# Layer 2 of a four-layer network: norms with pixels on partitions, rounds in a pinned order, work handed to GpSimd and ScalarE; layer 0: other PSUM banks for its first units

## The chip, the core and the metric

The kernel runs on one core of a Trainium2 chip, in one launch. The metric is the device time of that launch in microseconds (us). Three runs of the kernel before gave 16575.54, 16579.15 and 16581.78 us; their median is 16579.15 us. The engines are named as in the profile: PE (TensorE; PEld is its weight load), DVE (VectorE), ACT (ScalarE), POOL (GpSimd) and SP (SyncE, which only issues transfers here).

## The reference, cut to what matters

The network has four layers on a tensor of 4 images, 96 channels and 56 x 56 = 3136 pixels, fp32 throughout. Each layer is applied to a group norm of the tensor and added to it. The change touches layer 0 (full attention with 3 heads of 16 dimensions) and layer 2.

```python
# layer 0, per image and head
attn = jax.nn.softmax(jnp.einsum('bhnd,bhmd->bhnm', q, k) * scale, axis=-1)
out = jnp.einsum('bhnm,bhmd->bhnd', attn, v)

# layer 2 (input: the group norm of x), per pixel p and the 15 x 15 window around it
x_n = x_flat / jnp.maximum(jnp.linalg.norm(x_flat, axis=-1, keepdims=True), 1e-12)
sims = jnp.where(valid, einsum(x_n[p], x_n[window of p]), -1e9)
top_sim, top_idx = jax.lax.top_k(sims, 8)
wts = jax.nn.softmax(top_sim, axis=-1)
agg = sum over k of wts[k] * x_flat[top_idx[k]]
x_ln = (x_flat - mean) / jnp.sqrt(var + 1e-05) * ln_w + ln_b     # over the 96 channels
enhanced = agg + x_ln
h = jax.nn.relu(enhanced @ w1.T + b1)
out = enhanced + h @ w2.T + b2
```

## The kernel before

The layers run one after another; each opens its own pools of tiles and closes them at its end, so that the next layer starts when the last one is done. Layers 1 and 3 are untouched by the change and take most of the time.

**Layer 2** works image by image (`for b in range(B)`). An image lies in SBUF as 96 partitions (channels) by 3136 pixels; `CH` is 448 pixels (7 chunks), `KT` is 112 pixels, two image rows (28 tiles). An image goes through four stages:

1. Group norm (`group_norm`, lines 88 to 110): seven statistics instructions, two tiny matmuls that average over groups of channels, a square root on ACT, and one scaling pass into `xf`.
2. Norms over the channels, which lie on partitions, chunk by chunk (lines 912 to 940). A square on ACT (L915, L932), a matmul with a 96 x 96 matrix of ones, which leaves the sum on every partition (L917, L926, L934), a square root on ACT (L919, L936), a reciprocal of the whole 96 x 448 chunk on DVE (L922, L938), and products on DVE. The results are `unit` (vectors of length 1) and `enh` (the layer norm, to which the attention is added). Then seven groups of four PE transposes make `ft`, the image with pixels on partitions (L947, L950).
3. Attention, 28 tiles of 112 queries (lines 953 to 1002). A tile needs the keys of its own and up to four tiles on both sides: `nt` is 9 in the middle and 5 to 8 near the image's top and bottom. PE makes the scores (L963); DVE adds the window mask and takes them out of PSUM (L967), finds the eight largest (L972), makes a copy in which these are replaced by a very small number (`left`, L974) and negates the maximum (L976); ACT takes three exponentials (L979 with the sum of the eight, L980 of all scores, L981 of `left`); DVE subtracts the last two (L983), so that only the eight weights are left, and makes a diagonal matrix of one over the sum (L985, L987); PE turns the weights, nine blocks of 112 x 112, with that diagonal as the other operand (L993), ACT copies them out of PSUM (L996), PE sums the nine products with `ft` (L999), and DVE adds the result to `enh` (L1002).
4. The two-layer perceptron, seven chunks (L1008, L1011, L1014, L1016, L1017), and a store issued by POOL (L1018).

The order on each engine is not written out in layer 2: the program order is the loop's, and the scheduler of the framework rearranges it, within what the tiles' numbers of buffers allow (two for most, one for `unit`). PSUM has eight banks: `psS` two tiles of two banks for scores, `psT` two of one bank for the turned weights, `psM` two of one bank for all else.

**Layer 0** is under `in_order(tc)`, which chains each instruction to the one before it on the same engine, so that the order of the program is the order of each engine. A unit is 128 queries by 448 keys of one head for all four images. Its scores are four matmuls with 32 rows each (`score`, L196), image `b` in row group `b`; DVE takes the maximum of each query (`largest`: L210 for a tile of two banks at once, L208 for one bank). The first `LEAD` = 160 units run ahead of everything else. Images 0 and 1 make one pair, 2 and 3 the other: of three pairs in turn, two get a `psE` tile of two banks, and the third gets two single banks of `psM`.

```python
if places % 3 < 2:
    p = psE.tile([128, 2, 512], F32, name="s")
    two = [p[:, 0], p[:, 1]]
    ps.append((bs[0], p))
else:
    two = [bank() for _ in bs]
    ps += zip(bs, two)
```

After a unit with n % 4 == 2, a block of other work is put in, 23 in all: 16 times `values` (L162) and 7 times `project` (L181), both of which use `psM` banks, as does `into_row` (L223) once in seven units. `psE` has two tiles (four banks), `psM` three banks, and `psA` one bank, for the accumulator that is used after the first 160 units.

## Time and profile before

| what | value |
|---|---|
| median of three runs | 16579.15 us |
| the profiled execution, its own time | 16544.92 us |
| its span | 16543.1 us |
| layer 2, from its first loads to its last store (9504 to 10604) | 1100 us |
| the first 160 units of layer 0 (64 to 486) | 422 us |
| busy in layer 2: DVE / PE / ACT / POOL | 843 / 856 / 541 / 15 us |
| table loads of ACT in layer 2 | 39 of 1283 ns |
| granted PE clock, whole span / layer 2 / the first 160 units | 0.91 / 0.86 / 0.56 |

The profiled execution is 34 us (0.2%) shorter than the median of the runs. Durations are taken from it, and sums are made against its own time. In the tables of groups, a row gives the line, engine and operation, the tiles written and read with their shapes, the number of instructions, the busy time with the mean of one in ns, and the engine's idle time just before them with what ended it. In the timeline a row gives the start, the duration, engine, line and operation; neighbouring instructions of one kind are merged. The stretches (windows) give the busy time of each engine in a stretch of the span, then the granted PE clock as a share of full speed.

### The profile page before, as it was taken

How to read it: one execution, taken by the hardware profiler on the slowest of the kernel's cores; microseconds unless marked ns; L12 is line 12 of the kernel's file. 1: busy time of each engine (PE TensorE's matmuls, PEld its weight loads, DVE VectorE, ACT ScalarE, POOL GpSimd, SP SyncE). 2: the span in 40 equal slices, each digit the busy share in tenths (PEclk: the TensorE clock that was granted, in tenths of full speed). 3: DMA queues.
4: the chain of work that ended last, by engine and by line, in shares of the span. 5: the costliest groups of instructions: out<-in, count | busy, mean ns of one | idle time of the engine just before them, and what ended most of it. 6: DMA issues, size and time to landing. Idle time of an engine off the chain costs nothing.

```text
span 16543.1 us, 501276 instructions
## 1 busy us (share of the span) xinstructions
PE 13366.7 (81%) x221976; PEld 8983.6 (54%) x221976; DVE 13918.8 (84%) x15345; ACT 12240.4 (74%) x15452; POOL 7665.0 (46%) x3968
## 2 busy tenths in 40 slices
PE   8999977777777777777776678778888888888866
PEld 4333325666666666666665445446666656666533
DVE  7666549999999999999998777768888888888866
ACT  0465449999999999999996244468888888888822
POOL 0000028888888888888885000023333333333300
PEclk6899889999999999999998588889999999999977
DMA  0000034334444434344445800122212222221122
GB/s 15 1 1 1 16 137 97 91 92 95 105 105 103 103 91 96 92 96 102 103 105 139 194 10 10 43 71 51 50 47 50 50 50 51 51 50 47 43 66 66
DMA packets 821402, 1152.50 MB, mean 70 GB/s; under 512 B 309360, under 2 KB 728720, under 8 KB 807456
## 3 DMA queue, kind: packets, MB, share of 16 engines
q1 hardware_dynamic: 759872, 1055.38, 26.3%
q10 hardware_dynamic: 53984, 45.77, 1.2%
q8 instruction: 1745, 28.59, 0.8%
q0 software_dynamic: 5376, 19.27, 0.4%
q14 instruction: 425, 3.48, 0.1%
HBM read 842.93 MB, written 277.18 MB: 68 GB/s over the span
## 4 chain that ended last, share of the span: by engine, by line
PE 32%; DVE 28%; ACT 19%; issue 15%; DMA 5%; SPq 1%; POOL 1%; DVEq 0%; ACTq 0%; POOLq 0%
DVE q L638 17%; PE q L1357 7%; ACT ht L663 5%; PE s L233 4%; ACT e L626 3%; PE d L417 3%; ACT phi L1305 3%; DVE w L1345 3%; PE z L1297 2%; PE acc L251 2%; PE m L196 2%; ACT w L1313 2%; PE t L561 2%; PE y L675 2%; DVE phi L1366 2%
## 5 line engine op out<-in xcount | busy, mean ns | idle before, releaser
L618 POOL TENSOR_TENSOR q<-du,bm 128x1792 f32<-128x1792 f32 x1344 | 5345.3, 4024 | 3.1 <-DMA bm<-bc 3.1
L638 DVE TENSOR_TENSOR_SCAN q<-e,state,q 128x448 f32<-128x448 f32 x4608 | 4874.1, 1122 | 142.7 <-ACT e L626 140.1
L626 ACT ACTIVATE e<-dl,na 128x448 f32<-128x448 f32 x5376 | 3355.4, 640 | 179.4 <-DVE q L638 123.7
L675 PE MATMUL y<-ht,cd 128*32 128x64 f32 x75264 | 1836.6, 225 | 1480.0 <-ACT ht L663 1479.5
L654 PE MATMUL t<-ident,q 128*128 128x128 f32 x18816 | 2611.9, 292 | 93.9 <-issue 77.8
L1357 PE MATMUL q<-w,m 32*32 32x192 f32 x52224 | 2573.2, 348 | 124.1 <-DVE phi L1366 71.2
L654 PEld LDWEIGHTS t<-ident,q 128*128 128x128 f32 x18816 | 2377.1, 203 | 324.4 <-issue 201.1
L663 ACT COPY ht<-t 128x896 f32<-128x896 f32 x2688 | 2428.3, 903 | 87.1 <-PE t L654 57.1
L675 PEld LDWEIGHTS y<-ht,cd 128*32 128x32 f32 x75264 | 1399.7, 110 | 1958.2 <-ACT ht L663 1942.9
L1357 PEld LDWEIGHTS q<-w,m 32*32 32x32 f32 x52224 | 1873.3, 113 | 737.7 <-issue 184.3
L1366 DVE TENSOR_TENSOR phi<-q,phi 128x768 f32<-128x768 f32 x1632 | 1512.4, 952 | 519.4 <-PE q L1357 491.7
L1378 POOL TENSOR_TENSOR t<-t 128x384 f32<-128x384 f32 x408 | 407.3, 998 | 2974.2 <-DVE t L1377 2974.2
L1297 PE MATMUL z<-ad,sm 32*32 32x256 f32 x39168 | 1277.4, 391 | 396.2 <-ACT phi L1305 382.0
L241 ACT ACTIVATE e<-s 128x896 f32<-128x896 f32 (+1 forms) x1050 | 921.7, 915 | 902.6 <-PE m L196 508.2
L1305 ACT COPY phi<-z 128x1536 f32<-128x1536 f32 x816 | 1164.5, 1427 | 526.5 <-PE z L1297 526.3
L208 DVE TENSOR_REDUCE pm<-m 128x1 f32<-128x448 f32 (+1 forms) x1672 | 982.9, 616 | 667.1 <-PE m L196 599.6
L1345 DVE TENSOR_TENSOR w<-w,misc 128x3072 f32<-128x3072 f32 x408 | 1364.8, 3345 | 82.7 <-PE misc L1329 47.0
L1313 ACT ACTIVATE w<-phi,lntiny,w_k_rmask 128x3072 f32<-128x3072 f32 x408 | 1203.1, 2949 | 2.6
L196 PE MATMUL m<-ka,qa 32*128 32x448 f32 (+1 forms) x3344 | 1169.3, 638 | 7.5 <-DVE pm L208 7.5
L1321 ACT ACTIVATE phi<-phi,w_k_nmask 128x3072 f32<-128x3072 f32 x408 | 1165.5, 2857 | 2.4
L1297 PEld LDWEIGHTS z<-ad,sm 32*32 32x32 f32 x39168 | 708.7, 104 | 659.6 <-ACT phi L1305 463.0
L292 POOL DMA_DIRECT2D x<-xc x28 | 14.5, 517 | 2178.4 <-DVE xc L291 2177.5
(255 smaller groups left out, 18928.9 us busy)
## 6 DMA issues: line engine op xcount, KB each, us to landing
bm<-bc SPq DMA_DIRECT2D x896, 448.0 KB
cm<-cd SPq DMA_DIRECT2D x544, 186.0 KB
l1y<-out SPq DMA_DIRECT2D x672, 96.0 KB
l1y<-out SPq DMA_DIRECT2D x672, 72.0 KB
y<-l1y ACTq DMA_DIRECT2D x224, 168.0 KB
l3y<-y SPq DMA_DIRECT2D x1616, 23.2 KB
w<-l3cr SPq DMA_DIRECT2D x408, 48.0 KB
l3cr<-phi SPq DMA_DIRECT2D x408, 48.0 KB
```

The lines of the kernel that those rows point to most:

```text
L618: nc.gpsimd.tensor_tensor(q, spread(s["du"][:, j, :], ng), s["bm"][g], ALU.mult)
L626: nc.scalar.activation(e[:, :CH], s["dl"][:, j, :], AF.Exp, scale=na[:, s["k"], j, n : n + 1])
L638: nc.vector.tensor_tensor_scan(a, e, a, first, ALU.mult, ALU.add)
L654: nc.tensor.transpose(flat(t)[:, 128 * c : 128 * c + 128], view(q, h * NC2 + c, [[NC, 128]]), self.ident,)
L663: nc.scalar.copy(t, flat(s["t", j, g, h])[:, : NC2 * 128])
L675: nc.tensor.matmul(s["y", j][r : r + 32, c // 4, 64 * half : 64 * half + 64], s["cd"][:, half, g, c, :], s["t", j, g, h][:, 128 * i + 64 * ...
L1297: nc.tensor.matmul(z[32 * b : 32 * b + 32, p, dh].rearrange("p n d -> p (n d)"), s["s"][ps_, dh, b, lo : lo + 32], st["ad"][ps_, dh, 8 * h ...
L1305: nc.scalar.copy(st["phi"][:, :, :, 8 * h : 8 * h + 8, :].rearrange("p a b n d -> p a b (n d)"), z.rearrange("p a b n d -> p a b (n d)"),)
L1313: nc.scalar.activation(w.rearrange("p a n d -> p (a n d)"), st["phi"].rearrange("p a b n d -> p (a b n d)"), AF.Sigmoid, bias=lntiny, scal ...
L1345: nc.vector.tensor_tensor(st["w"], st["w"], ut, ALU.mult)
L1357: nc.tensor.matmul(qp[bs, n, :DI], st["m"][bs, 4 * q + n, :], st["w"][bs, :, 4 * q + n, :], start=True, stop=True,)
L1366: nc.vector.tensor_tensor(ph, view(st[q], 0, [[256, 4], [32, 6], [1, 32]]), ph, ALU.mult)
```

## The change

In layer 2 the stages become functions, and the whole layer is put under `in_order`. The norms are made with pixels on partitions: the group norm is transposed first, mean and variance of each pixel come from the statistics instructions of DVE over the 96 channels, the factors for 112 x 28 pixels are worked out in a few small instructions, ACT scales by one over the length (`fu`), DVE subtracts the mean and scales (`fl`), and PE transposes both back to `unit` and `enh`. The matrix of ones, its matmuls and the reciprocals of whole chunks are gone.

The attention runs in rounds over four tiles at different stages: in round k the scores of tile k + 1, the selection for tile k, the exponentials of tile k - 1, and the turning and summing of tile k - 2. The subtraction of the two exponentials is issued to POOL, the diagonal to ACT. The group norm of the next image comes after an image's last round, the first half of its other norms between the chunks of the perceptron, and the second half after the last chunk. The perceptron takes its PSUM tiles from `psS` and `psT`.

In layer 0, the first 160 units take banks by turns: an even unit both `psE` tiles, an odd one the three `psM` banks and the one of `psA`. The four scores of a unit are issued together.

In the diff, the lines taken out of layer 2 are left out; they stand in the listing above.

```diff
@@ -299,20 +299,16 @@
                     project(0, c)
                 between = [lambda b=b, t0=t0: values(b, t0) for t0 in range(0, NT, 8) for b in range(B)]
                 between += [lambda c=c: project(1, c) for c in range(NCH)]
-                places = 0
                 for n, u in enumerate(units[:LEAD]):
-                    ps = []
-                    for bs in pairs:
-                        if places % 3 < 2:
-                            p = psE.tile([128, 2, 512], F32, name="s")
-                            two = [p[:, 0], p[:, 1]]
-                            ps.append((bs[0], p))
-                        else:
-                            two = [bank() for _ in bs]
-                            ps += zip(bs, two)
-                        places += 1
-                        for b, p in zip(bs, two):
-                            score(u, b, p)
+                    if n % 2 == 0:
+                        ps = [(bs[0], psE.tile([128, 2, 512], F32, name="s")) for bs in pairs]
+                        four = [p[:, i] for _, p in ps for i in range(2)]
+                    else:
+                        four = [bank() for _ in range(3)] + [psA.tile([128, 512], F32, name="acc")]
+                        ps = list(enumerate(four))
+                    for b, p in enumerate(four):
+                        score(u, b, p)
                     for b, p in ps:
                         largest(u, b, p)
                     if ended:
@@ -883,6 +879,8 @@
     def layer2(self, xin, xout):
         nc, tc = self.nc, self.tc
         with ExitStack() as cx:
             wp = cx.enter_context(tc.tile_pool(name="l2w", bufs=1))
@@ -896,50 +894,22 @@
                 self.load(wp, f"l2_{n}") for n in ("w1", "b1", "w2", "b2", "lnw", "lnb")
             )
             mask = self.load(wp, "k_window")
...
             def misc():
                 return psM.tile([128, 512], F32, name="misc")
...
+            def fetch(b):
                 x = sp.tile([C, L], F32, name="x")
                 nc.sync.dma_start(x, xin[b])
...
+                return dict(b=b, x=x)
+            def norms(s):
+                xf = s1.tile([C, L], F32, name="xf")
+                self.group_norm(s["x"], xf, ss, psM, "misc")
+                ft = s["ft"] = sp.tile([KT, NKT, C], F32, name="ft")
+                mv = sp.tile([KT, NKT, 2], F32, name="mv")
+                yield
                 for t0 in range(0, NKT, 4):
                     p = misc()
                     for i in range(4):
@@ -950,72 +920,172 @@
                     nc.scalar.copy(
                         ft[:, t0 : t0 + 4, :], p[:KT, : 4 * C].rearrange("p (t c) -> p t c", c=C)
                     )
...
+                    for t in range(t0, t0 + 4):
+                        st = ss.tile([KT, 6], F32, name="st", bufs=4)
+                        nc.vector.bn_stats(st, ft[:, t, :])
+                        nc.vector.bn_aggr(mv[:, t, :], st)
+                    yield
+                mu, var = mv[:, :, 0], mv[:, :, 1]
+                rn = sp.tile([KT, NKT], F32, name="rn")
+                rs = sp.tile([KT, NKT], F32, name="rs")
+                nc.vector.tensor_tensor(rn, mu, mu, ALU.mult)
+                nc.vector.tensor_tensor(rn, rn, var, ALU.add)
+                nc.scalar.activation(rn, rn, AF.Sqrt, scale=float(C))
+                nc.scalar.activation(rs, var, AF.Sqrt, bias=self.eps[:KT])
+                nc.vector.tensor_scalar(rn, rn, 1e-12, None, ALU.max)
+                nc.vector.reciprocal(rn, rn)
+                nc.vector.reciprocal(rs, rs)
+                unit = s["unit"] = s1.tile([C, L], F32, name="unit")
+                enh = s["enh"] = sp.tile([C, L], F32, name="enh")
+                for t0 in range(0, NKT, 4):
+                    fu = ss.tile([KT, 4, C], F32, name="fu")
+                    fl = ss.tile([KT, 4, C], F32, name="fl")
+                    for i in range(4):
+                        t = t0 + i
+                        nc.scalar.mul(fu[:, i, :], ft[:, t, :], rn[:, t : t + 1])
+                        nc.vector.tensor_scalar(
+                            fl[:, i, :], ft[:, t, :], mv[:, t, 0:1], rs[:, t : t + 1],
+                            ALU.subtract, ALU.mult,
+                        )
+                    cs = slice(t0 * KT, (t0 + 4) * KT)
+                    for f, o in ((fu, unit), (fl, enh)):
+                        p = misc()
+                        for i in range(4):
+                            nc.tensor.transpose(
+                                p[:C, i * KT : (i + 1) * KT], f[:, i, :], self.ident[:KT, :KT]
+                            )
+                        if o is unit:
+                            nc.vector.tensor_copy(o[:, cs], p[:C, :CH])
+                        else:
+                            nc.scalar.activation(o[:, cs], p[:C, :CH], AF.Identity, bias=lnb, scale=lnw)
+                    yield
+            def tile_of(s, i):
+                t0, t1 = max(0, i - 4), min(NKT - 1, i + 4)
+                return dict(
+                    s=s, t0=t0, nt=t1 - t0 + 1, m0=(t0 - i + 4) * KT, qs=slice(i * KT, (i + 1) * KT),
+                )
+            def scores(q):
+                hn = q["nt"] * KT // 2
+                unit = q["s"]["unit"]
+                p = q["p"] = psS.tile([KT, 2, 512], F32, name="s")
+                for a in range(2):
+                    k0 = q["t0"] * KT + a * hn
+                    nc.tensor.matmul(
+                        p[:, a, :hn], unit[:, q["qs"]], unit[:, k0 : k0 + hn], start=True, stop=True
                     )
...
+            def select(q):
+                n, m0 = q["nt"] * KT, q["m0"]
+                sm = q["sm"] = ss.tile([KT, 9 * KT], F32, name="sm", bufs=4)
+                nc.vector.tensor_tensor(
+                    sm[:, :n].rearrange("p (a k) -> p a k", a=2), q["p"][:, :, : n // 2],
+                    mask[:, m0 : m0 + n].rearrange("p (a k) -> p a k", a=2), ALU.add,
+                )
+                top = q["top"] = ss.tile([KT, 8], F32, name="top", bufs=3)
+                nc.vector.max(top, sm[:, :n])
+                nb = q["nb"] = ss.tile([KT, 1], F32, name="nb", bufs=3)
+                nc.vector.tensor_scalar(nb, top[:, 0:1], -1.0, None, ALU.mult)
+                left = q["left"] = ss.tile([KT, 9 * KT], F32, name="left", bufs=3)
+                nc.vector.match_replace(left[:, :n], top, sm[:, :n], -1.0e30)
+            def first_exps(q):
+                n, sm = q["nt"] * KT, q["sm"]
+                et = ss.tile([KT, 8], F32, name="et")
+                tot = q["tot"] = ss.tile([KT, 1], F32, name="tot", bufs=3)
+                nc.scalar.activation(et, q["top"], AF.Exp, bias=q["nb"], accum_out=tot)
+                nc.scalar.activation(sm[:, :n], sm[:, :n], AF.Exp, bias=q["nb"])
+            def second_exps(q):
+                n, sm, left = q["nt"] * KT, q["sm"], q["left"]
+                nc.scalar.activation(left[:, :n], left[:, :n], AF.Exp, bias=q["nb"])
+                nc.gpsimd.tensor_tensor(sm[:, :n], sm[:, :n], left[:, :n], ALU.subtract)
+            def scale(q):
+                rt = ss.tile([KT, 1], F32, name="rt")
+                nc.vector.reciprocal(rt, q["tot"])
+                dg = q["dg"] = ss.tile([KT, KT], F32, name="dg", bufs=3)
+                nc.scalar.mul(dg, self.ident[:KT, :KT], rt)
+            def turned(q, a0):
+                if a0 == 0:
+                    q["wt"] = ss.tile([KT, 9, KT], F32, name="wt")
+                m = min(4, q["nt"] - a0)
+                if m <= 0:
+                    return
+                p = psT.tile([KT, 4, KT], F32, name="pt", padded_shape=[KT, 4, 128])
+                for a in range(m):
+                    at = (a0 + a) * KT
+                    nc.tensor.matmul(p[:, a, :], q["sm"][:, at : at + KT], q["dg"], start=True, stop=True)
+                nc.scalar.copy(q["wt"][:, a0 : a0 + m, :], p[:, :m, :])
+            def sums(q):
+                s, nt = q["s"], q["nt"]
+                p = misc()
+                for a in range(nt):
+                    nc.tensor.matmul(
+                        p[:C, :KT], s["ft"][:, q["t0"] + a, :], q["wt"][:, a, :],
+                        start=a == 0, stop=a == nt - 1,
+                    )
+                enh = s["enh"][:, q["qs"]]
+                nc.vector.tensor_tensor(enh, enh, p[:C, :KT], ALU.add)
+            def mlp(s, c):
+                cs = slice(c * CH, (c + 1) * CH)
+                enh = s["enh"][:, cs]
+                hid = ss.tile([C, 2, CH], F32, name="hid")
+                p = psS.tile([KT, 2, 512], F32, name="s")
+                for a in range(2):
+                    nc.tensor.matmul(p[:C, a, :CH], w1[:, a * C : (a + 1) * C], enh, start=True, stop=True)
+                    nc.scalar.activation(hid[:, a, :], p[:C, a, :CH], AF.Relu, bias=b1[:, a : a + 1])
+                p = psT.tile([KT, 512], F32, name="po", tag="pt")
+                for a in range(2):
+                    nc.tensor.matmul(p[:C, :CH], w2[:, a, :], hid[:, a, :], start=a == 0, stop=a == 1)
+                o = ss.tile([C, CH], F32, name="o")
+                nc.vector.scalar_tensor_tensor(o, p[:C, :CH], b2, enh, ALU.add, ALU.add)
+                nc.vector.tensor_tensor(o, o, s["x"][:, cs], ALU.add)
+                nc.gpsimd.dma_start(xout[s["b"]][:, cs], o)
+            with in_order(tc):
+                s = fetch(0)
+                for _ in norms(s):
+                    pass
+                for b in range(B):
+                    following = fetch(b + 1) if b + 1 < B else None
+                    qs = [tile_of(s, i) for i in range(NKT)]
+                    scores(qs[0])
+                    for k in range(NKT + 2):
+                        new, now, mid, old = (
+                            qs[j] if 0 <= j < NKT else None for j in (k + 1, k, k - 1, k - 2)
+                        )
+                        if new is not None:
+                            scores(new)
+                        if old is not None:
+                            scale(old)
+                        if now is not None:
+                            select(now)
+                        if mid is not None:
+                            first_exps(mid)
+                        if old is not None:
+                            turned(old, 0)
+                        if mid is not None:
+                            second_exps(mid)
+                        if old is not None:
+                            turned(old, 4)
+                            turned(old, 8)
+                            sums(old)
+                    coming = norms(following) if following is not None else iter(())
+                    next(coming, None)
+                    for c in range(NCH):
+                        mlp(s, c)
+                        next(coming, None)
+                    for _ in coming:
+                        pass
+                    s = following
     def into_layer3(self, xin, dram):
```

## The prediction

> **What bounds the kernel now.** The page came first: its slices show DVE at nine tenths from slice 7 to 21. That is layer 1, which the change leaves alone. So I read the two stretches that it touches, by busy time in windows: all of layer 2, a steady piece of its attention, a piece of its norms, and the first units of layer 0.
>
> ```profile
> 9504.00:10604.00 1100.00, 855.53 (x4680) 552.39 (x4680) 843.45 (x1313) 541.19 (x1019) 14.89 (x30) 0.86 0.04 10
> 9649.40:9730.30 80.90, 74.05 (x522) 55.12 (x522) 68.83 (x117) 44.89 (x92) 0.00 (x0) 1.00 0.00 1
> 9520.00:9600.00 80.00, 47.60 (x90) 20.56 (x90) 67.63 (x84) 34.47 (x60) 0.00 (x0) 0.63 0.00 0
> 64.00:486.00 422.00, 414.42 (x1643) 200.47 (x1640) 337.61 (x470) 17.03 (x33) 0.00 (x0) 0.56 0.00 1
> ```
>
> Columns: stretch, length, busy PE, PEld, DVE, ACT, POOL, then the granted clock. DVE is busiest in the norms, DVE and PE are close in the attention, POOL does nothing. Then layer 2's groups on DVE, ACT and PE, and the steady attention's waits:
>
> ```profile
> L983 DVE TENSOR_TENSOR sm<-sm,left 112x1008 f32<-112x1008 f32 (+4 forms) x112 | 124.2, 1115 | 14.6 <-ACT left L981 14.6
> L938 DVE RECIPROCAL rn<-nr 96x448 f32<-96x448 f32 x28 | 82.5, 2947 | 35.8 <-ACT nr L936 35.8
> L922 DVE RECIPROCAL rn<-nr 96x448 f32<-96x448 f32 x28 | 82.4, 2942 | 0.1
> L987 DVE TENSOR_SCALAR dg<-ident,rt 112x112 f32<-112x112 f32 x112 | 31.0, 277 | 3.5
> L979 ACT ACTIVATE et<-top,nb 112x8 f32<-112x8 f32 x112 | 33.7, 301 | 29.1 <-DVE nb L976 28.6
> L999 PE MATMUL misc<-wt,ft 112*96 112x112 f32 x1856 | 219.4, 266 | 39.8 <-ACT wt L996 38.7 <-ACT ft L950 0.8
> ```
> ```profile
> PE misc L999 <- ACT wt L996: 6.8, 13, 0.5
> DVE rt L985 <- ACT et L979: 11.2, 13, 0.9
> ```
>
> Thirteen tiles take 80.9 us, 6.22 each. Neither engine is full: DVE waits 0.86 us a tile for ACT's exponential, PE 0.52 us for ACT's copy. It is a ring of queues, and the timeline of PE and ACT shows its parts:
>
> ```profile
> 9683.04 1.86 PE L963 MATMUL s<-unit 96*112 96x504 f32 x4
> 9684.81 2.13 PE L993 MATMUL pt<-dg,sm 112*112 112x112 f32 x18
> 9685.91 0.53 ACT L996 COPY wt<-pt 112x448 f32<-112x448 f32 x1 [2.77 <-PE pt L993]
> 9686.78 0.93 PE L999 MATMUL misc<-wt,ft 112*96 112x112 f32 x8
> 9688.22 1.15 ACT L981 ACTIVATE left<-left,nb 112x1008 f32<-112x1008 f32 x1
> 9688.24 1.20 PE L999 MATMUL misc<-wt,ft 112*96 112x112 f32 x10 [0.52 <-ACT wt L996]
> 9689.27 1.86 PE L963 MATMUL s<-unit 96*112 96x504 f32 x4
> ```
>
> From start to start: scores 1.77 us, turning 1.97, first sums 0.93, wait 0.53, last sums 1.03. PE alone would need 5.70 us.
>
> **Layer 2: the attention round.** DVE loses L983 (1.20 us at full width) and L987 (0.28); ACT gains the diagonal, POOL the subtraction. No row shows ACT's diagonal. Bounds: the copy of 112x112 by ACT takes 0.26 us; the line from L979 (8 elements, 0.30) to L981 (1008, 1.15) gives 0.39 at 112. I take 0.38. It costs nothing while PE makes scores (1.77 us); without that cover it would cost all 0.38.
>
> The order on each engine is now fixed, so a full round can be laid out from the row intervals above, t = 0 at PE's start of the scores:
> - DVE: add of the last tile at 0.25, reciprocal 0.42 to 0.59. ACT: diagonal 0.62 to 1.0, exponentials of eight and of all scores until 2.34.
> - PE: scores until 1.77, turning from 1.77. As at 9684.81 and 9685.91, the first copy follows 1.10 later, at 2.87.
> - ACT: that copy's slot 0.43, so `left` at 3.30, slot about 1.05; second copy at 4.35, done 4.88. In the order of before the second copy went ahead of `left`; now it is queued behind it.
> - PE: turning ends 3.74, first sums until 4.67, waits for the copy until 4.93, last sums until 5.96.
>
> The round is 5.96 us against 6.22. DVE's own queue (0.17 + 0.14 + 1.23 + 1.2 + 0.1 + 1.2 + 0.17) is 4.2 us and waits about 1.8 for the sums: the bound is now PE with ACT. POOL starts after `left`, at about 4.5.
>
> **POOL's price: row or rule.** The nearest row is POOL's product in layer 1:
>
> ```profile
> L618 POOL TENSOR_TENSOR q<-du,bm 128x1792 f32<-128x1792 f32 x1344 | 5345.3, 4024 | 3.1 <-DMA bm<-bc 3.1
> ```
>
> That is 2.25 ns an element; shorter ones (L1337, 496 elements, 1167 ns) give 2.35. For 1008 elements 2.35 us, and the ends are 2.1 (L1338's 2.05 ns) and 2.6 (L1378's). The turning that needs it starts at 5.96 + 1.77 = 7.73, and 4.5 + 2.35 = 6.85: hidden, with 0.9 us to spare. The Trainium skill speaks against it: its page "Perfetto Trace Analysis", section "Optimizing Scalar/DVE Operations", says that GpSimd and DVE share an SBUF read port, and that moving operations between those two might not help. Taken at its worst, all of DVE's 4.2 us and POOL's 2.35 exclude each other: 6.55 us a round, 0.59 x 112 tiles = 66 us more than my sum. But L618 keeps its 2.25 ns beside DVE's scans (L638 idles 142.7 / 4608 = 0.03 us before each), and of DVE's instructions in a round the add and the last add read one operand from PSUM. I take the row.
>
> **An image's attention.** Before the first turning the pipeline fills: scores of tile 0 and 1, two selections on DVE (2.5 and 2.9 us), about 7.4 us. Then rounds with narrow old tiles (5 to 8) of 4.9, 5.2, 5.5 and 5.8, twenty of 5.96, then 5.6, 5.2 and two without new scores, 4.4 and 3.4: 159 us. The last stage leaves PE's clock low. At 9605 to 9610 of the trace the clock is 0.50 although PE is busy, and 1.00 from 9610: some 4 us at half speed, 2 us lost. Sum 168 us.
>
> **Between two images.** Nothing of this now runs beside attention, as some of it did.
> - Group norm up to its second small matmul: 5.9 us with PE empty (the same chain at 10615.7 to 10621.1 takes 5.4). The rest lies beside the perceptron.
> - Seven chunks, perceptron and transposes in one queue: 3.15 us for the matmuls (8 of 0.37, and a wait for the first L1011; alone the chunk took 3.48 with its order) and 0.5 for four transposes (four take 0.85 at half clock, 0.4 at full): 25.6 us, and 1.5 for the cold start. DVE beside it: 1.3 for L1016 and L1017, and four times statistics and their aggregation. Those of 112x192 take 0.338 and 0.169; for 96 columns, on the slope to 96x448 (0.608), 0.24 + 0.17 with a short wait, 0.42: 1.7. Together 3.0 of 3.65, hidden.
> - The last statistics 2.4 us, then the small instructions for 3136 factors, about 1.1. ACT needs one square-root table here, loaded ahead, in place of the many switches.
> - Second half, seven chunks: on ACT four scalings of 112x96 (bounds 0.26 as above and 0.39, slot 0.28) 1.2 us; transposes at half clock and latency 0.45; DVE's copy is beside it; transposes of `fl` 0.65 more; ACT's scaling out of PSUM, 0.65. Near 2.95 a chunk, 20.6 us, with nothing beside it.
> Together 57 us.
>
> **Sum of layer 2.** Loads as before 12; image 0 alone: group norm 8.3, statistics 13.4 (7 x 1.7 and a start), 1.1, 20.6, that is 43; four attentions 672; three stages between, 171; the last perceptron 24 (it took 25.7). Sum 922 us against 1098 to the last store: 175 saved. DVE's bill agrees in kind. Per image it had 211 us of work; 98 go (reciprocals 41.2, L983 31.0, L987 7.8, the products and maxima of the norms 18), 24 come (28 statistics pairs, 28 scalings, 7 copies).
> The stores stay on POOL's queue; they are issued in the perceptron, when no subtraction is left, so the 0.51 us of each costs nothing. The load of the next image moves ahead of the attention on SP's queue, where nothing else stands.
>
> **Layer 0.** DVE's two kinds of maximum, and why it idles:
>
> ```profile
> L210 DVE TENSOR_REDUCE pm<-s 128x2 f32<-128x896 f32 x214 | 224.5, 1083 | 69.0 <-PE s L196 37.7 <-PE m L196 31.3
> L208 DVE TENSOR_REDUCE pm<-m 128x1 f32<-128x448 f32 x212 | 121.4, 613 | 26.8 <-PE s L196 26.2 <-PE m L196 0.6
> ```
>
> Its idle 96 us are the 23 blocks: one of `values` holds PE 3.6 us and DVE then stands 4.28. Of 320 pairs, 214 were wide; now it is 160 wide and 320 single: 160 x 1.049 + 320 x 0.573 = 351 us against 346, 5 more. With eight banks in place of seven, a block finds about 1 us more of maxima already scored: 23 saved. `into_row`, after an odd unit, must wait for a bank just in use, 0.6 us eleven times: 7. Net 11 us saved. Bounds: 20 lost (no gain at the blocks and twice the waits), 35 saved. Counted as 10.
>
> **The forecast.** 175 + 10 = 185 us off the profiled 16544.9, 16360. The median of the runs stands 34 us higher, so 16579 - 185 = 16394.
>
> **Rivals.**
> *Half is delivered.* A fixed order cannot fill gaps. If rounds stay at 6.22 (0.26 x 112 = 30 less), the stage between images takes 85 us (3 x 28 = 84 less), image 0 loses 15 and layer 0 its 10, 45 us remain: 16534. For: before, the scheduler laid norms beside attention (DVE busy 85% at 9520 to 9600), and my chain of 3 us a chunk counts several crossings between engines. Against: those crossings show 0.03 to 0.2 us.
> *Slower.* One ring contains POOL: turning, first copy, `left`, subtraction, next turning. It takes 1.10 + 0.43 + 1.15 + 0.1 + S = 2.78 + S us. It passes the round of 5.96 when the subtraction takes S = 3.2, and eats all 185 us when the round grows by 185 / 112 = 1.65, at S = 4.83: twice the row. If POOL is blocked by DVE for whole instructions and S is 5.5, the round is 8.28, and the loss 112 x 2.32 - 185 = 75: 16654. For: the page cited. Against: row L618.
> *No change.* S near 4.8, or PE's clock held low through part of each attention by its waits of 0.26 us, would just consume the gain: 16579. Against: with waits of 0.52 us a tile the clock was 1.00.
>
> **How the numbers follow.** About 0.2% (33 us) is what this kernel's measurement can tell from no change. Forecast 0.74, its own range 16340 to 16450 (rounds of 5.70, PE's floor, to 6.2; layer 0's bounds; 2.6 to 3.6 us a norm chunk). Half delivered 0.15, of which 0.02 fall within 0.2%. Slower 0.07. No change 0.04. So faster 0.87, same 0.06, slower 0.07. The range runs from 16335 to 16505 and leaves out the far half of the second case and the last two.
>
> **What would show it.** In the changed profile: layer 2 near 922 us; wide rounds 5.96 us apart on PE, with a wait of about 0.26 for the second copy; POOL's subtraction at 2.35 us x112; DVE idle on PE's sums, not on ACT; 57 us between the last sums of an image and the next scores. I am wrong if POOL's rows exceed 3.2 us, if PE waits for POOL before turning, or if PE's clock is below 1.00 in the wide rounds.

## The result, and the profile after

| | before | changed |
|---|---|---|
| median of the runs | 16577.35 us | 16323.52 us |
| range | 16543.09 to 16581.78 us | 16312.18 to 16344.06 us |
| ratio, 95% interval | | 0.9856, 0.9842 to 0.9869 |
| span of the profiled execution | 16543.1 us | 16342.0 us |
| first 160 units of layer 0 | 421.4 us | 383.7 us |
| rest of layer 0 | 1716.1 us | 1729.1 us |
| layer 1 | 7302.3 us | 7305.9 us |
| layer 2, from its first loads to layer 3's | 1096.7 us | 916.3 us |
| layer 3 | 5942.6 us | 5943.0 us |

The changed kernel is faster. Its ratio of 0.9856 is 239 us (217 to 262); the medians of four runs each differ by 254 us, the two profiles by 201. The profile of before is of one of the shorter executions (16544.92 us), that of the changed kernel of the longest of its four (16344.06 us). Of the 201, layer 2 gives 180 and the first units of layer 0 give 38; the rest of layer 0, whose code is the same, took 13 us more in this execution, and layer 1 took 4 more.

The same four stretches as in the prediction, of the changed kernel (columns: stretch, length, busy PE, PEld, DVE, ACT, POOL, granted clock). First layer 2, then thirteen steady tiles, then the norms of image 0, then the first units of layer 0:

```profile
9482.70:10399.00 916.30, 768.29 (x4737) 541.15 (x4736) 568.11 (x1276) 517.32 (x1107) 254.78 (x140) 0.91 0.05 12
9568.90:9644.43 75.53, 72.39 (x522) 56.26 (x521) 51.84 (x91) 49.92 (x104) 30.11 (x14) 1.00 0.00 1
9487.00:9536.80 49.80, 19.73 (x88) 13.90 (x89) 28.04 (x109) 15.90 (x44) 0.00 (x0) 0.50 0.23 56
64.00:447.50 383.50, 358.49 (x1637) 188.04 (x1636) 338.44 (x519) 16.63 (x33) 0.00 (x0) 0.73 0.00 1
```

DVE lost 275 us of work in layer 2 (843 to 568), and 916 us passed all the same: nothing is full over the layer. The groups that answer to those shown of before, and TensorE's wait for GpSimd:

```profile
L1005 POOL TENSOR_TENSOR sm<-sm,left 112x1008 f32<-112x1008 f32 x80 | 185.3, 2316 | 275.5 <-ACT left L1004 275.5
L1011 ACT ACTIVATE dg<-ident,rt 112x112 f32<-112x112 f32 x112 | 43.4, 388 | 160.5 <-DVE rt L1009 160.5
L1035 DVE TENSOR_TENSOR enh<-enh,misc 96x112 f32<-96x112 f32 x112 | 29.9, 267 | 200.7 <-PE misc L1030 200.7
PE pt L1023 <- POOL sm L1005: 10.8, 12, 0.9
```

DVE idles before its last add, on TensorE (1.75 us in each wide round); GpSimd idles 3.5 us in one. TensorE waited for GpSimd 12 times, in the last three rounds of each image, where nothing new is scored. One wide round in the timeline:

```profile
9603.78 1.86 PE L975 MATMUL s<-unit 96*112 96x504 f32 x4
9605.47 2.08 PE L1023 MATMUL pt<-dg,sm 112*112 112x112 f32 x18
9606.51 0.53 ACT L1024 COPY wt<-pt 112x448 f32<-112x448 f32 x1 [0.46 <-PE pt L1023]
9606.94 1.14 ACT L1004 ACTIVATE left<-left,nb 112x1008 f32<-112x1008 f32 x1
9607.38 0.93 PE L1030 MATMUL misc<-wt,ft 112*96 112x112 f32 x8
9607.98 0.68 ACT L1024 COPY wt<-pt 112x448 f32<-112x448 f32 x2
9608.56 1.20 PE L1030 MATMUL misc<-wt,ft 112*96 112x112 f32 x10 [0.24 <-ACT wt L1024]
9609.59 0.59 PE L975 MATMUL s<-unit 96*112 96x504 f32 x1
```

The round is 5.81 us: scores 1.69, turning 1.91, sums 2.21 with the wait of 0.24 for the second copy inside. And the perceptron between two images, from one chunk's first matmul to the next chunk's:

```profile
9708.85 0.92 PE L1043 MATMUL s<-enh,w_l_w 96*96 96x448 f32 x2
9710.49 0.99 PE L1043 MATMUL s<-enh,w_l_w 96*96 96x448 f32 x2 [0.72 <-ACT hid L1044]
...
9713.35 0.92 PE L1043 MATMUL s<-enh,w_l_w 96*96 96x448 f32 x2
```

A chunk takes 4.5 us. TensorE stands before the second half of each hidden layer until ACT has read the first half out of the same tile.

### The profile page after: what moved, and what is told of

Its sections match the earlier page's. It is cut to its first block, busy times and chain, and to the rows that moved or that the text cites. A ratio compares the mean times of both kernels' runs of the same rounds, so it can differ in the third digit from the quotient of the medians.

```text
span 16342.0 us, 501766 instructions
## 1 busy us (share of the span) xinstructions
PE 13255.0 (81%) x222032; PEld 8983.5 (55%) x222032; DVE 13647.4 (84%) x15363; ACT 12214.4 (75%) x15540; POOL 7905.1 (48%) x4079
## 4 chain that ended last, share of the span: by engine, by line
PE 34%; DVE 29%; ACT 20%; issue 12%; DMA 4%; POOL 1%; SPq 1%; DVEq 0%; ACTq 0%; POOLq 0%
DVE q L634 17%; PE q L1427 7%; ACT ht L659 5%; PE s L233 4%; ACT e L622 3%; PE d L413 3%; ACT phi L1375 3%; DVE w L1415 3%; PE z L1367 2%; PE acc L251 2%; PE m L196 2%; ACT w L1383 2%; PE y L671 2%; PE t L557 2%; PE t L650 2%
```

## The experiments

The table has what the profiles of all kernels show of layer 2; the attention runs from an image's first scores to its last, "between" from there to the next image's first scores (means of four and of three). The same layer 2 takes 916.3 and 920.0 us in two profiles (changed, layer 2 alone), the old one 1096.7 and 1095.6: differences of this size say nothing. The runs are compared by their ratios to the kernel before, which ran beside each of them.

| kernel | layer 2 | attention | between | wide round | ratio (95%) |
|---|---|---|---|---|---|
| before | 1096.7 | | | 6.22 | 1 |
| changed | 916.3 | 141.3 | 83.1 | 5.81 | 0.9856 (0.9842 to 0.9869) |
| layer 2 alone | 920.0 | | | | 0.9884 (0.9869 to 0.9899) |
| layer 0 alone | 1095.6 | | | | 0.9975 (0.9965 to 0.9985) |
| work back on DVE | 920.2 | 142.8 | 82.6 | 5.81 | 0.9864 (0.9850 to 0.9877) |
| norms alone | 907.5 | 160.9 | 61.9 | 6.22 | 0.9894 (0.9880 to 0.9907) |
| norms and the two moves, old loop | 909.4 | 160.4 | 62.6 | 6.10 | 0.9881 (0.9868 to 0.9895) |
| scheduler orders layer 2 | 739.6 | 135.1 | 42.9 | 5.33 | 0.9763 (0.9743 to 0.9783) |
| the same, work back on DVE | 752.8 | 138.8 | 42.5 | 5.33 | 0.9766 (0.9752 to 0.9779) |
| subtraction twice | 1130.3 | 185.8 | 91.7 | 7.54 | 0.9978 (0.9969 to 0.9988) |
| two tiles for the hidden halves | 886.5 | 141.3 | 75.2 | 5.81 | 0.9831 (0.9817 to 0.9844) |
| exponentials first | 911.0 | 138.4 | 83.4 | 5.57 | 0.9842 (0.9829 to 0.9856) |
| pinned, norms spread | 854.2 | 140.8 | 65.2 | | 0.9817 (0.9804 to 0.9831) |
| scheduler, norms spread | 728.8 | 133.8 | 41.4 | | 0.9748 (0.9734 to 0.9761) |

### The two layers apart

Layer 2's part alone keeps the old first units of layer 0; layer 0's part alone keeps the old layer 2. In the first:

```diff
-                    if n % 2 == 0:
-                        ps = [(bs[0], psE.tile([128, 2, 512], F32, name="s")) for bs in pairs]
...
+                        if places % 3 < 2:
+                            p = psE.tile([128, 2, 512], F32, name="s")
```

> The changed layer 2 with layer 0 as it was. Theory (the two parts add; layer 2 gives about 180 us of the span, layer 0 about 38 in its first 160 units, and the rest of layer 0 differs only by the clock it is granted): about 180 us less than before, so near 1.1% (ratio 0.989); layer 2 from its first loads to its last store 917 us, the first 160 units 421 us. Rival (the gain of layer 0 is an accident of the clock, and all of the measured 239 us comes from layer 2): ratio 0.986.

> Layer 2 as before, layer 0's first 160 units in all banks by turns. Theory: the first 160 units take 384 us in place of 421, because the clock of PE rises with the four scores issued together and the blocks become shorter; ratio 0.9977 (38 us), give or take 15 us for the clock in the rest of layer 0. Rival (what the prediction said: half clock stays, 10 us): 0.9994. Rival (the rest of layer 0 loses what the first units gain): 1.000.

Layer 2 alone: 16354.44 us, ratio 0.9884, layer 2 of 920.0 us. Layer 0 alone: 16514.84 us, ratio 0.9975, which is 41 us (25 to 58). The gains in the ratio, 0.0116 and 0.0025, add up to 0.0141 against 0.0144 of both: the parts add up. Layer 0's part is four times what the prediction counted.

DVE's groups in these first units say where it comes from; those of before are shown in the prediction. The changed kernel's:

```profile
L210 DVE TENSOR_REDUCE pm<-s 128x2 f32<-128x896 f32 x159 | 165.6, 1084 | 17.9 <-PE s L196 17.9
L208 DVE TENSOR_REDUCE pm<-m 128x1 f32<-128x448 f32 x237 | 133.8, 618 | 38.9 <-PE m L196 35.8 <-PE s L196 2.9
L208 DVE TENSOR_REDUCE pm<-acc 128x1 f32<-128x448 f32 x79 | 48.7, 616 | 0.0
```

A maximum takes as long as before. DVE's idle time before them fell from 96 to 57 us (17.9 + 38.9), while the granted clock of the stretch rose from 0.56 to 0.73. The stretch was 409 to 425 us in the four profiles with the old banks (clock 0.55 to 0.62) and 376 to 386 us in the ten with the new ones (0.72 to 0.76). Counted in the two timelines, the idle time at the 23 blocks fell from 74 to 35 us. The blocks hold TensorE for 52 us in all, where they held it for 66: of the twelve full ones of `values`, eleven took 3.5 us or more before and four after, the rest of those 2.0 to 2.8.

### The two moves to GpSimd and ACT, in the pinned order

```diff
-                nc.gpsimd.tensor_tensor(sm[:, :n], sm[:, :n], left[:, :n], ALU.subtract)
+                nc.vector.tensor_tensor(sm[:, :n], sm[:, :n], left[:, :n], ALU.subtract)
...
-                nc.scalar.mul(dg, self.ident[:KT, :KT], rt)
+                nc.vector.tensor_scalar(dg, self.ident[:KT, :KT], rt, None, ALU.mult)
```

> The changed kernel with the subtraction of the exponentials and the diagonal issued to DVE again, in the same places of the pinned order. Theory (in the pinned round DVE waits 1.75 us for PE's sums, and the round is set by PE and ACT): DVE's queue grows from 4.2 to about 5.6 us and still fits in 5.81, the subtraction ends at about 5.7 of the round instead of 6.9, and the narrow last rounds of an image no longer wait for POOL (0.9 us, 12 times); so the same time within 15 us as the changed kernel, ratio to before 0.985 to 0.987. Rival (the work taken off DVE is what made the change faster): the round becomes 6.2 to 7.2 us, 40 to 150 us slower than the changed kernel, ratio 0.989 to 0.995.

16328.82 us, ratio 0.9864 against 0.9856: no difference that the runs can tell. The round stays at 5.81 us. DVE's subtraction (1198 ns at full width) and the diagonal go into its idle time before the last add, which falls from 200.7 to 41.2 us. Two of its groups in this kernel:

```profile
L988 DVE MAX8 top<-sm 112x8 f32<-112x1008 f32 x80 | 96.9, 1211 | 2.7
L1035 DVE TENSOR_TENSOR enh<-enh,misc 96x112 f32<-96x112 f32 x112 | 29.8, 266 | 41.2 <-PE misc L1030 40.4
```

Layer 2 is 4 us longer in the profile, no more than two profiles of one program differ. The moves bought nothing that shows here, since DVE did not bound the round.

### GpSimd's ring

```diff
+                twin = ss.tile([KT, 9 * KT], F32, name="twin", bufs=1)
+                nc.gpsimd.tensor_tensor(twin[:, :n], sm[:, :n], left[:, :n], ALU.subtract)
                 nc.gpsimd.tensor_tensor(sm[:, :n], sm[:, :n], left[:, :n], ALU.subtract)
```

> The changed kernel with GpSimd's subtraction run twice (first into a scratch tile, then the real one): GpSimd is busy 4.6 us in a round of 5.81 us, so it still has room as an engine. Theory of the ring (2.78 us of other work plus the time S of the subtraction, S = 4.6): the round becomes 7.4 us, which is 1.6 us in each of 80 wide rounds and about 0.7 in 32 narrow ones, 150 us in all; layer 2 about 1066 us, ratio 0.995. Rival, GpSimd counts as an engine only: 4.6 is below 5.81, the round stays at 5.8 to 6.0, layer 2 at 916 to 940, ratio 0.986 to 0.987.

16517.07 us, ratio 0.9978, layer 2 of 1130.3 us. The kernel's timeline, one round:

```profile
9600.33 1.14 ACT L1004 ACTIVATE left<-left,nb 112x1008 f32<-112x1008 f32 x1
9601.54 2.32 POOL L1006 TENSOR_TENSOR twin<-sm,left 112x1008 f32<-112x1008 f32 x1 [2.83 <-ACT left L1004]
9603.94 2.32 POOL L1007 TENSOR_TENSOR sm<-sm,left 112x1008 f32<-112x1008 f32 x1
9606.31 1.82 PE L1025 MATMUL pt<-dg,sm 112*112 112x112 f32 x16 [1.48 <-POOL sm L1007]
9607.87 1.14 ACT L1004 ACTIVATE left<-left,nb 112x1008 f32<-112x1008 f32 x1
```

From the first subtraction's start to the turning it is 4.77 us. From the turning to the next `left` it is 1.56, and from `left` to the subtraction 1.21, together 2.77: the ring that the prediction priced at 2.78 + S, with 7.54 us a round. It had said that S = 4.83 eats the whole gain; at 4.77 layer 2 is 34 us longer than before the change, about what layer 0 gains. GpSimd is busy 4.6 of 7.5 us. So an engine with over a third of its time free sets the pace, by its latency in the ring. The loss of 214 us against 150 expected comes from narrow rounds and the drained rounds too (the stretch between images grew by 8.6 us). With one subtraction the ring would need an estimated 2.77 + 2.4 = 5.2 us (half of the 4.77 for S) and stays below the round of 5.81.

### The norms alone, and the two moves in the old loop

The norms alone are put into the kernel before, whose loop, buffers and scheduler stay; the other kernel adds the two moves. From the one to the other:

```diff
-                    nc.vector.tensor_tensor(sm[:, :n], sm[:, :n], left[:, :n], ALU.subtract)
+                    nc.gpsimd.tensor_tensor(sm[:, :n], sm[:, :n], left[:, :n], ALU.subtract)
...
-                    nc.vector.tensor_scalar(dg, self.ident[:KT, :KT], rt, None, ALU.mult)
+                    nc.scalar.mul(dg, self.ident[:KT, :KT], rt)
```

> The kernel before with only the norms of layer 2 made with pixels on partitions; loop, order by the scheduler, subtraction and diagonal as before. Theory (the norms give most of it: DVE's bill per image falls from 211 to about 155 us, and the scheduler still lays what it can beside the attention): 100 to 150 us less, ratio 0.991 to 0.994. Rival (the pinned order gives most): less than 60 us, ratio over 0.9965.

> The kernel before with the new norms (layer 2 of 907.5 us, a round of 6.22 us, scheduler's order) and the two moves to GpSimd and ScalarE, its old loop otherwise: one unit's instructions written after the other's, two buffers of each tile. Layer 0 is that of before. Theory A, the old loop keeps a unit's chain on the path: GpSimd's 2.3 us in the place of VectorE's 1.2 us lengthen the round by 1.1 us to 7.3 us, layer 2 takes 1000 to 1030 us, ratio 0.995 to 0.998. Theory B, the moves alone free VectorE: the round falls to 5.3 to 5.6 us and layer 2 to 740 to 800 us, ratio 0.979 to 0.983.

The norms alone: 16376.68 us, ratio 0.9894, a gain of some 175 us where 100 to 150 were expected. Layer 2 takes 907.5 us, 189 less than before and 9 less than with the whole change; the runs do not tell it from layer 2's whole part (0.9884). The timeline of its TensorE shows that the attention's round is that of before, 6.23 us with the wait of 0.52, but that a chunk of the perceptron takes 3.48 us:

```profile
9640.89 1.86 PE L966 MATMUL s<-unit 96*112 96x504 f32 x4
...
9646.08 1.20 PE L1002 MATMUL misc<-wt,ft 112*96 112x112 f32 x10 [0.52 <-ACT wt L999]
9647.12 1.86 PE L966 MATMUL s<-unit 96*112 96x504 f32 x4
...
9724.94 1.93 PE L1011 MATMUL misc<-enh,w_l_w 96*96 96x448 f32 x4
...
9728.42 1.93 PE L1011 MATMUL misc<-enh,w_l_w 96*96 96x448 f32 x4
```

So the pinned loop and the moves together won 0.41 us in each wide round, 78 us over the four attentions, and lost it again: 64 us between the images, 19 before the first scores, 4 at the end. The moves in the old loop: 16353.00 us, layer 2 of 909.4 us, a mean round of 6.10 (its tiles run in pairs, 12.2 us for two). Both theories missed: neither 1.1 us lost nor the round freed. The waits of seven of its double rounds show the trade; columns are total in us, times, longest:

```profile
DVE sm L970 <- PE pt L996: 16.0, 7, 3.0
PE pt L996 <- POOL sm L986: 10.1, 14, 2.0
```

TensorE now waits for GpSimd before each turning, and DVE waits for TensorE to give back `sm`, of which there are two.

### The order left to the scheduler

```diff
-            with in_order(tc):
+            if True:
                 s = fetch(0)
```

> The changed kernel, with layer 2 left to the scheduler in place of the pinned order; everything else stays (norms with pixels on partitions, GpSimd's subtraction, ScalarE's diagonals, layer 0). Theory: what the order gains in a round of attention (5.81 us against 6.22 in the kernel with the norms alone) it gives back in the MLP (4.5 us against 3.44 a chunk) and in the first rounds, which the scheduler lets run beside the norms. Then layer 2 takes 905 to 935 us against 916, and the ratio to the kernel before is 0.985 to 0.988 (changed kernel 0.986). Rival: without the order TensorE waits for GpSimd's subtraction in each of the 112 rounds (2.3 us against 1.2 on VectorE): a round of 7 us or more, layer 2 over 990 us, ratio 0.991 or more.

> The changed kernel's layer 2 left to the scheduler, as in the kernel whose order was left to the scheduler (layer 2 of 739.6 us, a round of 5.33 us), but with the subtraction and the diagonal back on VectorE. Theory A: with the order free TensorE sets the round (5.33 us), and VectorE with four wide passes of 1.2 us, the diagonal and the small ones (1.0 us) comes to 5.8 us and becomes the bound; the round is 5.8 us, layer 2 takes 775 to 800 us, ratio 0.978 to 0.980: the two moves to GpSimd and ScalarE are then worth some 50 us, which the pinned order had hidden. Theory B, the moves made all the difference between 907.5 us (norms alone, old loop) and 739.6 us: layer 2 is about 907 us, ratio 0.986. Theory C, they are worth nothing here either: 735 to 750 us, ratio 0.976.

The first takes 16159.61 us, ratio 0.9763, far outside what both theories allowed: the same instructions take 739.6 us in layer 2 in place of 916.3. The windows of the changed kernel, then of this one: the norms of image 0, and the stretch from its last scores to the next image's first.

```profile
9482.70:9536.80 54.10, 19.75 (x89) 13.90 (x89) 28.66 (x110) 15.90 (x44) 0.51 (x1) 0.50 0.25 59
9678.10:9760.60 82.50, 57.44 (x254) 32.03 (x253) 43.58 (x142) 36.17 (x83) 9.03 (x11) 0.81 0.12 30
```
```profile
9423.10:9457.50 34.40, 8.82 (x45) 6.94 (x45) 21.58 (x96) 7.44 (x22) 0.51 (x1) 0.50 0.37 93
9593.30:9636.30 43.00, 38.84 (x212) 24.07 (x211) 26.31 (x104) 23.98 (x53) 7.89 (x9) 0.95 0.20 52
```

Over the layer, the start gives 20 us, four attentions 25, three stretches between images 121, and the end 12: 177. Between images TensorE is busy 39 of 43 us, where it was busy 57 of 82: the perceptron starts in the last rounds, the next image's norms run beside it, its first scores run between the transposes of the norms, and the clock is 0.95 in place of 0.81. Four rows of TensorE's timeline, two of each seam:

```profile
9605.06 0.92 PE L1043 MATMUL s<-enh,w_l_w 96*96 96x448 f32 x2
9605.82 1.12 PE L1030 MATMUL misc<-wt,ft 112*96 112x112 f32 x10
...
9636.27 1.14 PE L975 MATMUL s<-unit 96*112 96x280 f32 x2
9637.20 0.95 PE L954 MATMUL misc<-ident,fl 112*96 112x112 f32 x4
```

L1043 is the perceptron, L1030 still the last tile's sums; L975 is the first scores, L954 the norms' transposes.

A round of its attention, from the timeline of all engines:

```profile
9541.27 1.86 PE L975 MATMUL s<-unit 96*112 96x504 f32 x4
9542.73 1.12 ACT L1004 ACTIVATE left<-left,nb 112x1008 f32<-112x1008 f32 x1
9542.97 2.08 PE L1023 MATMUL pt<-dg,sm 112*112 112x112 f32 x18
9543.93 2.34 POOL L1005 TENSOR_TENSOR sm<-sm,left 112x1008 f32<-112x1008 f32 x1 [3.00 <-ACT left L1004]
9544.04 0.51 ACT L1024 COPY wt<-pt 112x448 f32<-112x448 f32 x1
9544.41 1.21 DVE L988 MAX8 top<-sm 112x8 f32<-112x1008 f32 x1
9544.74 0.69 ACT L1024 COPY wt<-pt 112x448 f32<-112x448 f32 x2 [0.19 <-PE pt L1023]
9544.88 1.89 PE L1030 MATMUL misc<-wt,ft 112*96 112x112 f32 x18
9546.61 1.86 PE L975 MATMUL s<-unit 96*112 96x504 f32 x4
```

The exponential `left` runs ahead of both copies, TensorE waits for nothing, and the 18 sums run in one piece: 1.73 us in place of 2.21. DVE's MAX8 lies wholly beside GpSimd's subtraction and takes 1.21 us, as it does with GpSimd idle (1211 ns in the kernel with the work back on DVE).

With the subtraction and the diagonal back on DVE this order takes 16165.64 us, ratio 0.9766 against 0.9763, and 752.8 us in layer 2: 13 us more in the profile, which the medians do not show. Theory C came nearest. A had added up whole durations, 5.8 us a round. In this kernel's timeline DVE's wide passes last 1.19 to 1.20 us, but the next instruction starts 1.11 us after a pass did, and a round of its work takes 5.0 to 5.15 us. That is just under TensorE's 5.33, as this stretch of wide rounds shows, with both engines full:

```profile
9520.00:9580.00 60.00, 60.00 (x453) 47.65 (x452) 59.62 (x108) 41.87 (x83) 0.00 (x0) 1.00 0.00 1
```

So the moves would count as soon as TensorE's round became shorter. With the 907.5 and 909.4 us of the old loop this makes a square: the new loop (four tiles at different stages, the next image's norms written between the chunks of the perceptron, more buffers of `sm`, `left` and `dg`, other PSUM tiles for the perceptron) is worth 155 and 170 us when the scheduler orders it, the two moves -2 and 13.

### Repairs within the pinned order

Two PSUM tiles for the hidden halves:

```diff
-                p = psS.tile([KT, 2, 512], F32, name="s")
                 for a in range(2):
+                    p = psS.tile([KT, 2, 512], F32, name="s")
-                    nc.tensor.matmul(p[:C, a, :CH], w1[:, a * C : (a + 1) * C], enh, start=True, stop=True)
+                    nc.tensor.matmul(p[:C, 0, :CH], w1[:, a * C : (a + 1) * C], enh, start=True, stop=True)
...
```

> The changed kernel, with the two hidden halves of an MLP chunk in two PSUM tiles in place of the halves of one. Theory: the second half's matmul waits 0.72 to 0.78 us for ScalarE's relu of the first half only because both lie in one tile; with two tiles the chunk falls from 4.5 to 3.5 to 3.8 us, 28 chunks give 20 to 28 us, layer 2 takes 888 to 897 us, ratio 0.984 to 0.985. Rival: ScalarE's own two relus (0.63 us each with their start) or the bank being used set the pace; the chunk stays above 4.3 us and nothing is gained.

16270.76 us, ratio 0.9831, layer 2 of 886.5 us, 30 less and a little more than expected. Its timeline has the four rows of both halves in one piece, without the wait, and 3.6 us a chunk:

```profile
9647.50 1.67 PE L1043 MATMUL s<-enh,w_l_w 96*96 96x448 f32 x4
...
9651.11 1.67 PE L1043 MATMUL s<-enh,w_l_w 96*96 96x448 f32 x4
```

Exponentials ahead of the copies, and the ninth turned tile from `psM`:

```diff
-                        if old is not None:
-                            turned(old, 0)
                         if mid is not None:
                             second_exps(mid)
                         if old is not None:
+                            turned(old, 0)
                             turned(old, 4)
...
```

> The changed kernel, with ScalarE taking both exponentials ahead of the turning copies in each round, and the ninth turned tile in a PSUM tile of the other pool. Theory: the 0.24 us that TensorE waits in a round for the copy of the turned weights goes, and the round falls from 5.81 to 5.55 to 5.65 us; 112 rounds give 15 to 28 us, ratio 0.984 to 0.985. Rival: the copies come 1.1 us later behind the exponentials and TensorE waits for them instead: a round of 6.0 us or more, 20 us or more lost, ratio 0.987 or more.

16296.38 us, ratio 0.9842 against 0.9856, which is unclear. The round is 5.57 us as expected, but layer 2 is only 5 us shorter (911.0). The attentions of the first two images gained 4.1 us each, which would be 16 for four, within the 15 to 28 expected. The other two gained less, at a clock of 0.98 and 0.97, and the last stretch took 5.5 us more at a clock of 0.87, where it was 1.00 in the changed kernel: this profile's clock hides most of the gain.

The norms spread, once pinned (with both repairs) and once left to the scheduler (with the two tiles):

```diff
+                    early = first_half(following) if following is not None else []
                     scores(qs[0])
                     for k in range(NKT + 2):
+                        some, more = early[k - 6] if 0 <= k - 6 < len(early) else (None, None)
...
```

> The changed kernel with its order still pinned, but three things moved in it: the exponentials ahead of the turning copies (a round of 5.57 us in the run with that alone), two PSUM tiles for the hidden halves (886.5 us of layer 2 against 916), and the first half of the next image's norms spread over rounds 6 to 20 of this image's attention. Theory: the loss of the pinned order lies in what it forbids to overlap between images; spreading takes 15 to 20 us from each of three stretches between images, so layer 2 takes 916 - 5 - 30 - 50 = 830 us, at most 15 us off, ratio 0.980 to 0.982. Rival: the spread steps delay the rounds they are put into (each has VectorE, TensorE and ScalarE work) by as much as they save: layer 2 stays at 875 to 890 us, ratio 0.983 to 0.984.

> The changed kernel with the order left to the scheduler, two PSUM tiles for the hidden halves, and the first half of the next image's norms written into rounds 6 to 20. Theory: with the order free, TensorE is the bound (a round of 5.33 us without waits) and what is left to gain are its waits between images, some 10 to 15 us each: layer 2 takes 700 to 730 us against 739.6, ratio 0.974 to 0.976. Rival: the spread work only takes TensorE's, ScalarE's and VectorE's time in the rounds: 735 to 760 us, ratio 0.976 to 0.978.

Pinned: 16251.20 us, layer 2 of 854.2 us, between the two theories: the stretch between images fell to 65.2 us (75.2 with the two tiles alone), but the rounds that carry the steps gave back some 2 us an image. Left to the scheduler: 16140.21 us, ratio 0.9748, layer 2 of 728.8 us, as expected. It and the kernel without the spread are both faster than the kernel before and the changed one; between these two the intervals overlap.

## Why the prediction was right or wrong

**Layer 2's sum.** 175 us were predicted and 180 measured, but the terms were off in both directions: that the sum came so near is partly luck.

| term | predicted | profile |
|---|---|---|
| first loads and norms of image 0 | 12 + 43 | 54.1 |
| four attentions, to the last sums | 4 x 168 | 4 x 158.7 |
| three stretches between images | 3 x 57 | 3 x 65.7 |
| last perceptron and store | 24 | 30.3 |

The round was laid out as 5.96 us with a wait of 0.26 for the second copy, and ran in 5.81 with 0.24; the scores took 1.69 us, not 1.77, and ACT followed a little sooner. The attention was over-counted by 9 us: 5 in the twenty wide tiles (119.2 counted, 114.4 in the timeline, since the last of them have narrower tiles beside them), 3.5 in the narrow tiles at both ends, and 2 counted for a slow clock at the start; the fill itself took 7.9 us, not 7.4. The chunk of the perceptron was the step that failed: 3.65 us predicted, 4.5 measured. Seven chunks held the stretch for 34.8 us, where 25.6 + 1.5 were counted, and that is nearly all of its 8.7 us; the group norm ahead of them (5.9) and the second half of the norms (20.0 for 20.6) came as laid out. The sum had counted the matmuls and one wait; the diff showed that both halves now lie in one tile, and the second matmul waits for the reader of the first. Two tiles brought the chunk to 3.6 us.

**GpSimd.** 2.35 us were predicted, 2.316 measured. The subtraction is hidden in wide rounds, as the prediction had it. One of its signs of being wrong, TensorE waiting for GpSimd, did come up in the twelve drained rounds; it cost 10.8 us in all. The row that the price came from was right, and the worst case that the prediction priced at 66 us from the Trainium skill's page "Perfetto Trace Analysis", section "Optimizing Scalar/DVE Operations", did not come: a MAX8 beside a subtraction was as fast as one without. The page's sentence is narrower than that case: it ties the lock on the shared port to a DVE operation that uses two ports. No instruction of DVE in these rounds reads two full tensors from SBUF, so for such a one the runs say nothing. What the page says of the worth, that such moves might not help, did hold in this order, for another reason: DVE had 1.75 us to spare in a round. The ring that would have made the kernel slower exists, 2.77 + S, and it took twice the subtraction to make it the bound.

**Layer 0.** 10 us were predicted, 38 measured from profile to profile and 41 (25 to 58) by the runs. Two terms failed. The step "a block finds about 1 us more of maxima already scored: 23 saved" took TensorE's clock of 0.56 as given, and with it the 3.6 us of a block. The clock rose to 0.73, the blocks became 14 us shorter, and the idle time at them fell by 39 us. The other 25 are near the 23 counted, but a faster clock can be in them too: with the old banks that idle time was 76, 74, 63 and 62 us at clocks of 0.55, 0.56, 0.59 and 0.62. The other term is `into_row`, priced at 7 us lost: the waits behind it went from 8 us to 5. (The prediction gave all 96 us of idle time to the blocks; 14 of them are the wait for the first scores, and 8 those behind `into_row`.) The 5 us of extra work for single banks came as 4, DVE's time in all 426 maxima against that in all 480; the stretch shown ends before the last five. Whether the clock rose because the four scores are issued together, or because of the eighth bank, no run here tells apart.

**What the order was worth.** The prediction laid the shorter round out from the moves and the fixed order together ("the order on each engine is now fixed") and put the order's price into a rival: "a fixed order cannot fill gaps". The rival's 85 us a stretch were too many (66 measured), but its mechanism is what the runs show: the norms alone save as much of layer 2 (189 us) as the whole change (180), and with the same instructions left to the scheduler it saves 357. So the forecast's 175 came out for a sum whose parts were credited wrongly: the norms give all of it, and what the pinned loop gained in a round it paid back between the images and before the first. The moves had no part in the shorter round: it stays at 5.81 us without them. What the new loop does without the order was not asked, and that is as large as the whole gain in layer 2: 177 us.

**The profile's own scatter.** The forecast of 185 us is 54 short of the 239 of the ratio, but 16 short of the 201 between the profiles, where its terms can be looked up. A short execution of before and a long one of the changed kernel were profiled; 13 of the missing 38 us lie in the rest of layer 0 (see below). So the 239 us are not accounted for term by term.

## What to carry to other kernels

Price a pinned order against the same program without it: it is a choice of its own, and here it cost 177 us, about what the new loop is worth without it. What it forbids lies at the seams, between images and before the first round, so lay the seam out as carefully as the steady round. And ask of any work that is moved off an engine whether that engine sets the round: here DVE lost 1.5 us of work a round, and the round did not notice.

## What the runs showed of the hardware that was not expected

The rest of layer 0 has the same instructions in every kernel, with TensorE 99% busy, and took 1661 to 1731 us in the fourteen profiles. It goes with the granted clock, 0.96 to 0.92: length times clock is 1589 to 1597 us in all of them. The windows of the pinned kernel with spread norms, then of the one with the norms alone.

```profile
447.60:2108.50 1660.90, 1645.59 (x11749) 568.14 (x11748) 977.98 (x1725) 940.59 (x1085) 13.97 (x27) 0.96 0.02 6
```
```profile
473.10:2203.60 1730.50, 1714.97 (x11748) 581.85 (x11748) 976.36 (x1721) 940.71 (x1085) 13.96 (x27) 0.92 0.02 6
```

A clock of 0.96 against 0.92 makes 70 us, with the same code and TensorE as busy. What grants it stays open. So before two single profiles of this kernel are compared, look first at the stretches that the change leaves alone.
